# Self-attention of a decoder block: score tiles of half a PSUM bank for three of four heads, and two groups of heads projected together

## The chip, the cores and the metric

The kernel runs on one core of a Trainium2 chip. The metric is the device time of one execution in microseconds (us). TensorE (PE) multiplies matrices, VectorE (DVE) and ScalarE (ACT) read the products out of PSUM, GpSimd (POOL) and SyncE (SP) help with element-wise work and transfers. PSUM here is used as eight banks, each of 128 partitions by 512 fp32 values.

## The reference

One decoder block on x of shape (2, 1024, 256): self-attention with 16 heads of 16, cross-attention over 77 context rows, and a mixture of 8 experts. Only the self-attention is touched by the change:

```python
q, k, v = heads(xn @ Wq), heads(xn @ Wk), heads(xn @ Wv)     # xn = layernorm(x)
attn = softmax(einsum('bhqd,bhkd->bhqk', q, k) * e ** -0.5)
out = einsum('bhqk,bhkd->bhqd', attn + rel_bias, v)
x = x + layernorm(out) * gamma + beta
```

## The kernel before

All values are fp32. The kernel runs in stages: normalise and transpose x, the values and the part of the output that comes from the relative bias (`bias_o`), then the self-attention (about 90 to 710 us), the cross-attention, the routing and the experts.

Heads come in groups of four. A head has 16 values, and is padded to 32 rows (`wpad`), so four heads fill the 128 rows of TensorE's array: head `hh` of a group sits in rows 32·hh to 32·hh+31, its *row group*, and matmuls on different row groups can run beside each other. A unit is one group of one batch row, `u = 0..7`. `project(u, name)` makes its queries (`wqT`) and keys (`wkT`), 128 x 1024, with four matmuls of 512 columns each (L416), read out by ACT (L425) and DVE (L427). Row 16 of each head is 1 in the keys; in the queries it will hold minus the largest score, so that the second score matmul gives scores that are already shifted for the exponential.

A unit is worked in two halves of 512 queries (`halves`), and a half in eight steps. TensorE's order is written by hand: a loop over `n` in which stream A works on step `n` and stream B on step `m = n - LAG`, ten steps later.

- `stream_a(n, p)`: scores of 128 queries against 512 keys for heads 2p and 2p+1 (L443, two matmuls into a tile `sA` of two banks); DVE takes the maximum over the keys (L450).
- `shift_queries(h)`: after eight steps, four transposes into `pm` (L462), and DVE adds the negated maxima to the queries in place (L466).
- `stream_b(m, p)`: scores with keys as rows, 128 keys against 512 queries, for heads 2p and 2p+1 (L478), one bank `sB` each; ACT takes the exponential into `pt` (L488).
- `times_v(m)`: four matmuls (L499) that add the products with the values and with a row of ones into the bank `av`; it works on what stream B of the step before made.
- `collect(h)`: every eight steps, four transposes (L518) into `po`, division by the sum (L521, L522), and the bias part (L529). After the last group of a half `affine_residual` normalises.

There are 128 steps of A and 128 of B. In the 118 steps that hold both, the order on TensorE is A for heads 0, 1; B for heads 2, 3; B for heads 0, 1; A for heads 2, 3; then the products with the values. PSUM holds two `big` tiles of two banks (`sA`, and `pp` of the projections), three banks `one` (`sB`, `pm`, `po`) and one bank for `av`. The tile framework adds the waits: a matmul that reuses a bank waits until the reader of the old contents has finished, and a reader waits until TensorE's semaphore has counted far enough. TensorE has one such semaphore for all its readers.

Of the kernel before, what the change touches and what calls it, by code (L numbers as in the profile page):

```python
# [14 lines left out]
P = 128  # L15
# [22 lines left out]
def decoder_kernel(  # L38
# [36 lines left out]
        return psum.enter_context(tc.tile_pool(name=name, bufs=bufs, space=bass.MemoryType.PSUM))  # L75


    ps2, ps1, psav = banks("ps2a", 2), banks("ps1a", 3), banks("psav", 1)

    def big(name):  # L80
        return ps2.tile([P, 2, 512], F32, tag="big", name=name)

    pair = big

    def one(name):
        return ps1.tile([P, 512], F32, tag="one", name=name)

    flip = [0]

# [27 lines left out]
    def load_bcast(src, name):  # L117
# [4 lines left out]
    ident = const.tile([P, P], F32, name="ident")  # L122
    make_identity(nc, ident)

    onescol = const.tile([P, 1], F32, name="onescol")
    nc.vector.tensor_reduce(
        onescol, ident.rearrange("p (g r) -> p g r", r=32)[:, :, 16], AX.X, ALU.add
    )
    nhalf = const.tile([P, NT], F32, name="nhalf")
    nc.gpsimd.memset(nhalf, -0.5)  # L130

# [68 lines left out]
    fst = first.enter_context(tc.tile_pool(name="fst", bufs=1))  # L200

    wv = load_rows(a_wv, "wv", D, fst)
    wpad = {}
    for name, src in (("wq", a_wq), ("wk", a_wk)):
        raw = load_rows(src, f"{name}raw", D, fst)
        pad = at1.tile([P, 2, H, 32], F32, name=f"{name}pad")
        nc.gpsimd.memset(pad, 0.0)
        nc.gpsimd.tensor_copy(pad[:, :, :, 0:DH], raw.rearrange("p kc (h d) -> p kc h d", h=H))
        wpad[name] = pad.rearrange("p kc h r -> p kc (h r)")
    gamma_a = load_bcast(a_gamma, "gamma_a")  # L210
    beta_a = load_bcast(a_beta, "beta_a")

# [40 lines left out]
    vaug = at1.tile([P, QT, H, 32, B], F32, name="vaug")  # L253
    nc.gpsimd.memset(vaug, 0.0)
    nc.gpsimd.memset(vaug.rearrange("p k h r b -> p (k h) r b")[:, :, DH, :], 1.0)
    shifts = []
    for i in range(2):
        m = at1.tile([P, 4, NG, 32], F32, name=f"shift{i}")
        nc.gpsimd.memset(m, 0.0)
        shifts.append(m)  # L260

    for c in range(4):
        normalized_T(c, xnT[:, :, 512 * c : 512 * c + 512])
# [95 lines left out]
    evacuate(cxT.rearrange("p kc b t -> p kc (b t)"), pc[:, :, : B * T2])  # L359
    kbd = const.tile([P, 2, B, 4, T2], F32, name="kbd")  # L360
    for G in range(2):
        pk = one("pk")
        for kc in range(2):
            nc.tensor.matmul(
                pk[:, : B * T2],
                lhsT=cwk[:, kc, P * G : P * G + P],
                rhs=cxT[:, kc, :, :].rearrange("p b t -> p (b t)"),
                start=(kc == 0),
                stop=(kc == 1),
            )  # L370
        for j in range(4):
            nc.vector.tensor_scalar(
                kbd[:, G, :, j, :],
                pk[:, : B * T2].rearrange("p (b t) -> p b t", b=B),
                hsel[:, j : j + 1],
                None,
                ALU.mult,
            )
    vx = const.tile([P, B, H, 2, DH], F32, name="vx")
    nc.gpsimd.memset(vx, 0.0)  # L380
    for b in range(B):
        pv = one("pcv")
        for kc in range(2):
            nc.tensor.matmul(
                pv[:T2, :D],
                lhsT=cxT[:, kc, b, :],
                rhs=cwv[:, kc, :],
                start=(kc == 0),
                stop=(kc == 1),
            )  # L390
        for i in range(2):
            nc.vector.tensor_copy(
                vx[:T2, b, i::2, i, :],
                pv[:T2, :D].rearrange("p (h i d) -> p i h d", i=2, d=DH)[:, i, :, :],
            )
# [6 lines left out]

    halves = [(b, g, qb) for b in range(B) for g in range(NG) for qb in range(2)]
    units = {}
    outs = {}

    def project(u, name):
        b, g = u // NG, u % NG  # L410
        dst = at2.tile([P, S], F32, tag=f"{name}T", name=f"{name}T{u}", bufs=3)
        units[u, name] = dst
        pp = pair("pp")
        for half in range(2):
            for kc in range(2):
                nc.tensor.matmul(  # L416
                    pp[:, half, :],
                    lhsT=wpad[name][:, kc, P * g : P * g + P],
                    rhs=xnT[:, kc, b * S + 512 * half : b * S + 512 * half + 512],
                    start=(kc == 0),  # L420
                    stop=(kc == 1),
                )
        pf = pp.rearrange("p a f -> p (a f)")
        if name == "wq":
            nc.scalar.copy(dst, pf)  # L425
        else:
            nc.vector.tensor_scalar(dst, pf, onescol[:, 0:1], None, ALU.add)  # L427

    largest = {}

    def stream_a(n, p):
        h, r = n // 8, n % 8
        b, g, qb = halves[h]
        u = h // 2
        if (r, p) == (0, 0):
            largest[h] = at2.tile([P, 4, 4, 2], F32, tag="mx", name=f"mx{h}", bufs=3)
        qt, half = r // 2, r % 2
        qT, kT = units[u, "wq"], units[u, "wk"]
        s = pair("sA")
        for j in range(2):  # L440
            r0 = 32 * (2 * p + j)
            q0 = 512 * qb + P * qt
            nc.tensor.matmul(  # L443
                s[:, j, :],
                lhsT=qT[r0 : r0 + 32, q0 : q0 + P],
                rhs=kT[r0 : r0 + 32, 512 * half : 512 * half + 512],
                start=True,
                stop=True,
            )
        nc.vector.tensor_reduce(  # L450
            largest[h][:, qt, 2 * p : 2 * p + 2, half], s, AX.X, ALU.max
        )

    def shift_queries(h):
        b, g, qb = halves[h]
        shift = shifts[h % 2]
        nc.vector.tensor_reduce(
            shift[:, :, :, DH], largest.pop(h), AX.X, ALU.max, negate=True
        )
        pm = one("pm").rearrange("p (t f) -> p t f", f=P)  # L460
        for t in range(4):
            nc.tensor.transpose(  # L462
                pm[:, t, :], shift[:, t, :, :].rearrange("p h r -> p (h r)"), ident
            )
        qh = units[h // 2, "wq"][:, 512 * qb : 512 * qb + 512]
        nc.vector.tensor_tensor(qh, qh, pm.rearrange("p t f -> p (t f)"), ALU.add)  # L466

    powers = {}

    def stream_b(m, p):  # L470
        h, kt = m // 8, m % 8
        b, g, qb = halves[h]
        qT, kT = units[h // 2, "wq"], units[h // 2, "wk"]
        tiles = []
        for j in range(2):
            r0 = 32 * (2 * p + j)
            s = one("sB")
            nc.tensor.matmul(  # L478
                s,
                lhsT=kT[r0 : r0 + 32, kt * P : (kt + 1) * P],  # L480
                rhs=qT[r0 : r0 + 32, 512 * qb : 512 * qb + 512],
                start=True,
                stop=True,
            )
            tiles.append(s)
        for j, s in enumerate(tiles):
            pt = atp.tile([P, 512], F32, tag="pt", name="pt")
            nc.scalar.activation(pt, s, AF.Exp, scale=1.0 / 16.0)  # L488
            powers[m, 2 * p + j] = pt

    sums = {}

# [18 lines left out]
    def collect(h):  # L511
        b, g, qb = halves[h]
        if (b, qb) not in outs:
            outs[b, qb] = kp.tile([P, 4, D], F32, tag="o", name=f"o{b}{qb}", bufs=4)
        o, avs = outs[b, qb], sums.pop(h)
        po = one("po").rearrange("p (t f) -> p t f", f=P)
        for t in range(4):
            nc.tensor.transpose(po[:, t, :], avs[:, t * P : (t + 1) * P], ident)  # L518
        po = po.rearrange("p t (h r) -> p t h r", r=32)
        rs = small.tile([P, 4, 4], F32, tag="rs", name="rs")  # L520
        nc.vector.reciprocal(rs, po[:, :, :, DH])  # L521
        nc.vector.tensor_tensor(  # L522
            o[:, :, 64 * g : 64 * g + 64].rearrange("p t (h d) -> p t h d", h=4),
            po[:, :, :, 0:DH],
            rs.unsqueeze(3).to_broadcast([P, 4, 4, DH]),
            ALU.mult,
        )
        og = o[:, :, 64 * g : 64 * g + 64]
        nc.gpsimd.tensor_tensor(  # L529
            og, og, bias_o[:, b, 4 * qb : 4 * qb + 4, 64 * g : 64 * g + 64], ALU.add  # L530
        )
        if g == NG - 1:
            c = 2 * b + qb
            affine_residual(o, xs[:, 4 * c : 4 * c + 4, :], c, gamma_a, 1e-3)

    steps = 8 * len(halves)
    with tc.manual_schedule(engines={nc.tensor.engine}):
        for n in range(steps + LAG + 4):
            m = n - LAG
            if n == 0:  # L540
                project(0, "wq")
                project(0, "wk")
            if n % 16 == 11 and n // 16 + 1 < B * NG:
                project(n // 16 + 1, "wq")
            if n % 16 == 13 and n // 16 + 1 < B * NG:
                project(n // 16 + 1, "wk")
            if n % 8 == 1 and 8 < n < steps + 8:
                shift_queries(n // 8 - 1)
            if n < steps:
                stream_a(n, 0)  # L550
            if 0 <= m < steps:
                stream_b(m, 1)
                stream_b(m, 0)
            if n < steps:
                stream_a(n, 1)
            if 1 <= m <= steps:
                times_v(m - 1)
            if m % 8 == 2 and 0 < m < steps + 8 and m // 8 >= 1:
# [570 lines left out]
```

## Time and profile before

| | |
|---|---|
| time, median of 2 runs (lowest, highest) | 1391.63 us (1389.13, 1394.13) |
| time of the profiled execution | 1389.76 us |
| span of its profile | 1388.0 us |
| PE, DVE, ACT, POOL busy | 1182.9, 630.2, 460.1, 255.6 us |
| mean granted TensorE clock | 0.918 |

Each fp32 matmul leaves two records on PE, one for each of its passes; a transpose leaves one. PEld are the loads of the stationary operand. A record on PE lasts longer than the pass holds the array, since its end is the end of the last result; so records overlap, and a PE that looks busy all the time can still be waiting. Times of a stretch are given in us from the start of the span.

### The profile page before, as it was taken

The page shows a single profiled execution, that of the slowest core. Times are in us where ns is not written, and L with a number is a line of the kernel's source. Part 1 is how long each engine was busy: PE and PEld are TensorE (multiplying, and loading weights), DVE is VectorE, ACT ScalarE, POOL GpSimd, SP SyncE. Part 2 cuts the span into 40 slices and gives each one's busy share as a digit, 9 for nine tenths or more (in the row PEclk, how much of TensorE's full clock was granted, in tenths as well). Part 3 has the DMA queues.
Part 4 walks back from the last instruction along what each step waited for, and adds up shares of the span by engine and source line. Part 5 has one row for each costly group of instructions (what it writes and reads, how often), then busy time and mean ns, then how long its engine had stood idle before and what let it go on. Part 6 is the DMA issues. An engine that isn't in the chain of part 4 may idle for free. (4 is left out here: it accounts for less than half of the span.)

```text
span 1388.0 us, 15187 instructions
## 1 busy us (share of the span) xinstructions
PE 1182.9 (85%) x6231; PEld 632.9 (46%) x6231; DVE 630.2 (45%) x903; ACT 460.1 (33%) x801; POOL 255.6 (18%) x225
## 2 busy tenths in 40 slices
PE   0889999999989999999966678865999999999950
PEld 0533333332323233333213445634788888888840
DVE  6326565656565656566338565544300100100117
ACT  0100454545444455545531434310222222222210
POOL 7200000000000000000015554612222322222111
PEclk9995999999999999999997888765999999999985
DMA  7000000000000000000000000005244554455223
GB/s 167 9 1 0 1 1 1 1 1 0 1 0 1 0 1 0 1 0 1 0 0 1 0 11 5 31 16 182 68 148 154 180 186 155 161 196 165 97 72 110
DMA packets 62149, 73.95 MB, mean 53 GB/s; under 512 B 18059, under 2 KB 53504, under 8 KB 62080
## 3 DMA queue, kind: packets, MB, share of 16 engines
q1 hardware_dynamic: 55632, 60.56, 13.0%
q0 software_dynamic: 4960, 11.29, 2.7%
q10 hardware_dynamic: 1488, 1.13, 0.3%
q8 instruction: 49, 0.80, 0.2%
q14 instruction: 20, 0.16, 0.0%
HBM read 64.31 MB, written 10.22 MB: 54 GB/s over the span
## 5 line engine op out<-in xcount | busy, mean ns | idle before, releaser
L450 DVE TENSOR_REDUCE mx<-sA 128x2 f32<-128x1024 f32 x256 | 313.2, 1224 | 194.3 <-PE sB L478 103.7
L478 PE MATMUL sB<-wqT,wkT 32*128 32x512 f32 x1024 | 380.2, 639 | 5.4 <-ACT pt L488 5.4
L488 ACT ACTIVATE pt<-sB 128x512 f32<-128x512 f32 x512 | 278.3, 597 | 298.2 <-PE sB L478 269.7
L443 PE MATMUL sA<-wkT,wqT 32*128 32x512 f32 x1024 | 301.9, 684 | 10.1 <-DVE mx L450 6.7
L478 PEld LDWEIGHTS sB<-wqT,wkT 32*128 32x128 f32 x1024 | 120.6, 186 | 164.6 <-ACT pt L488 103.1
L1046 PE MATMUL po<-w,hT 128*128 128x256 f32 x736 | 168.1, 382 | 11.2 <-DVE y L1055 11.2
L1036 ACT ACTIVATE hT<-ph,b1s 128x256 f32<-128x256 f32 x184 | 87.3, 474 | 245.8 <-PE ph L1029 245.1
L1029 PE MATMUL ph<-xgT,w 128*128 128x256 f32 x736 | 163.2, 380 | 0.4 <-DVE xgT L1022 0.4
L1055 DVE TENSOR_SCALAR y<-po,by 128x256 f32<-128x256 f32 x46 | 20.1, 480 | 311.1 <-PE po L1046 311.1
L1046 PEld LDWEIGHTS po<-w,hT 128*128 128x128 f32 x736 | 138.1, 190 | 34.1 <-DVE y L1055 16.1
L1029 PEld LDWEIGHTS ph<-xgT,w 128*128 128x128 f32 x736 | 132.6, 189 | 27.4 <-ACT hT L1036 3.6
L499 PE MATMUL av<-pt,vaug 128*32 128x512 f32 x1024 | 137.8, 611 | 0.0
L443 PEld LDWEIGHTS sA<-wkT,wqT 32*128 32x128 f32 x1024 | 80.8, 194 | 115.8 <-issue 77.8
L529 POOL TENSOR_TENSOR o<-o,bias_o 128x256 f32<-128x256 f32 x16 | 11.6, 724 | 649.2 <-DVE o L522 649.2
L1058 POOL DMA_INDIRECT pairs<-y,to_row x46 | 46.4, 1008 | 148.4 <-DMA pairs<-y,to_row 97.5
L1004 POOL DMA_INDIRECT xg<-xnd,from_row x46 | 44.8, 975 | 150.1 <-PE px L1018 126.0
L499 PEld LDWEIGHTS av<-pt,vaug 128*32 128x32 f32 x1024 | 20.6, 109 | 97.6 <-issue 97.4
L166 PE MATMUL pxT<-ident,xn 128*128 128x128 f32 x96 | 19.8, 359 | 48.3 <-DVE xn L156 45.5
L633 PE MATMUL ppT<-ident,st 128*77 128x128 f32 x256 | 37.9, 310 | 17.2 <-POOL st L622 16.9
L634 ACT COPY PT<-ppT 77x1024 f32<-77x1024 f32 x32 | 31.1, 1008 | 43.8 <-PE ppT L633 43.8
L633 PEld LDWEIGHTS ppT<-ident,st 128*77 128x77 f32 x256 | 33.7, 171 | 25.0 <-POOL st L622 19.3
L615 POOL TENSOR_TENSOR st<-st,cm 128x1232 f32<-128x1232 f32 x16 | 36.1, 2259 | 47.9 <-DVE cs L621 18.1
(202 smaller groups left out, 958.6 us busy)
## 6 DMA issues: line engine op xcount, KB each, us to landing
w<-in_L_ffn_W_dram SPq DMA_DIRECT2D x46, 1024.0 KB, 8.4
yt<-pairs SPq DMA_DIRECT2D x8, 512.0 KB, 4.8
xs<-in_x_dram SPq DMA_DIRECT2D x4, 512.0 KB, 6.4
xnd<-xn SPq DMA_DIRECT2D x4, 512.0 KB, 2.8
out_dram<-acc SPq DMA_DIRECT2D x4, 512.0 KB, 3.0
xg<-xnd,from_row POOLq DMA_INDIRECT x46, 2.7
pairs<-y,to_row POOLq DMA_INDIRECT x46, 2.5
mk<-in_mask_BxSxS_ik_dram SPq DMA_DIRECT2D x1, 616.0 KB, 8.5
```

The lines of the kernel that those rows point to most:

```text
L443: nc.tensor.matmul(s[:, j, :], lhsT=qT[r0 : r0 + 32, q0 : q0 + P], rhs=kT[r0 : r0 + 32, 512 * half : 512 * half + 512], start=True, stop=True,
L450: nc.vector.tensor_reduce(largest[h][:, qt, 2 * p : 2 * p + 2, half], s, AX.X, ALU.max)
L478: nc.tensor.matmul(s, lhsT=kT[r0 : r0 + 32, kt * P : (kt + 1) * P], rhs=qT[r0 : r0 + 32, 512 * qb : 512 * qb + 512], start=True, stop=True,)
L488: nc.scalar.activation(pt, s, AF.Exp, scale=1.0 / 16.0)
L499: nc.tensor.matmul(sums[h][32 * hh : 32 * hh + 32, :], lhsT=vaug[:, kt, 4 * g + hh, :, b], rhs=powers.pop((m, hh)), start=(kt == 0), stop= ...
L615: nc.gpsimd.tensor_tensor(st, st, cm.unsqueeze(2).to_broadcast([P, H, T2]), ALU.subtract)
L633: nc.tensor.transpose(pp[:T2, h, :], st[:, 8 * G + h, :], ident)
L1004: nc.gpsimd.indirect_dma_start(out=xg[:, s, :], out_offset=None, in_=xnd[:, :], in_offset=bass.IndirectOffsetOnAxis(ap=from_row[:, 2 * i + ...
L1029: nc.tensor.matmul(ph[:, j, :], lhsT=w1[:, kc, hc * P : (hc + 1) * P], rhs=xgT[:, kc, :], start=(kc == 0), stop=(kc == 1),)
L1036: nc.scalar.activation(hT[:, hc, :], ph[:, j, :], AF.Gelu, bias=b1s[:, i, hc : hc + 1])
L1046: nc.tensor.matmul(po[:, s, :], lhsT=hT[:, hc, s * P : (s + 1) * P], rhs=w2[:, hc, :], start=(hc == 0), stop=(hc == NH - 1),)
L1058: nc.gpsimd.indirect_dma_start(out=pairs[:, :], out_offset=bass.IndirectOffsetOnAxis(ap=to_row[:, k : k + 1], axis=0), in_=y[:, s, :], in_ ...
```

## The change

1. **Projection.** `project(w, name, j)` serves two groups of heads at once (`w = 0..3`) in four pieces of 256 columns for the queries and four for the keys. The 32 rows of a row group hold one head of each of the two groups, 16 rows each (`wqk`). A piece is two matmuls of 256 columns. Queries are copied once (`qc`); of the keys DVE makes two copies, one for each group, in which the other group's rows are 0 but for one row of ones (`own`, `extra`). The eight pieces of the next `w` are spread over every second step of 16 steps in 32.
2. **Half banks.** One of the three banks `one` stays; the other two become `hb0` and `hb1`. `halfbank()` deals out their four halves of 256 columns in turn: first half of `hb0`, first half of `hb1`, second half of `hb0`, second half of `hb1`. Projection pieces, `pm`, `po` and most of stream B take their PSUM from there.
3. **Stream B.** For heads 1, 2 and 3 a score tile of 512 queries becomes two of 256 queries, with a matmul and an exponential each. Head 0 keeps the whole bank.
4. **Order.** The step's order on TensorE is written out as `turns`, in which A and B alternate matmul by matmul.
5. **Shift and collect** work in two parts of 256 columns. The shifted queries go to tiles of their own (`qB`) instead of in place.

```diff
-    ps2, ps1, psav = banks("ps2a", 2), banks("ps1a", 3), banks("psav", 1)
+    ps2, ps1, psh, psav = banks("ps2a", 2), banks("ps1a", 1), banks("psh", 1), banks("psav", 1)
+    halfbanks = [psh.tile([P, 512], F32, name=f"hb{i}") for i in range(2)]
+    turn_of = [0]
+    def halfbank(name):
+        k = turn_of[0] % 4
+        turn_of[0] += 1
+        return halfbanks[k % 2][:, 256 * (k // 2) : 256 * (k // 2) + 256]
...
-        pad = at1.tile([P, 2, H, 32], F32, name=f"{name}pad")
-        nc.gpsimd.memset(pad, 0.0)
-        nc.gpsimd.tensor_copy(pad[:, :, :, 0:DH], raw.rearrange("p kc (h d) -> p kc h d", h=H))
+        w = at1.tile([P, 2, 2, 4, 2, DH], F32, name=f"{name}2")
+        for kc in range(2):
+            for G in range(2):
+                nc.gpsimd.tensor_copy(
+                    w[:, kc, G],
+                    raw[:, kc, P * G : P * G + P].rearrange("p (i h d) -> p h i d", i=2, h=4),
+                )
...
+    def project(w, name, j):
+        b, G = w // 2, w % 2
+        cols = slice(256 * j, 256 * j + 256)
+        pp = halfbank("pp")
+        for kc in range(2):
+            nc.tensor.matmul(
+                pp,
+                lhsT=wqk[name][:, kc, P * G : P * G + P],
+                rhs=xnT[:, kc, b * S + 256 * j : b * S + 256 * j + 256],
+                start=(kc == 0),
+                stop=(kc == 1),
+            )
+        if name == "wq":
...
+            nc.scalar.copy(units[w, "q"][:, cols], pp)
+            return
+        for i in range(2):
...
+            nc.vector.tensor_scalar(
+                units[w, "k", i][:, cols], pp, own[i][:, 0:1], extra[i][:, 0:1], ALU.mult, ALU.add
+            )
...
+    def stream_b(m, hh, part):
+        h, kt = m // 8, m % 8
+        b, g, qb = halves[h]
+        r0 = 32 * hh
+        s, cols = (one("sB"), slice(0, 512)) if part is None else (halfbank("sB"), slice(256 * part, 256 * part + 256))
+        nc.tensor.matmul(
+            s,
+            lhsT=units[h // 4, "k", g % 2][r0 : r0 + 32, kt * P : (kt + 1) * P],
+            rhs=shifted[h][r0 : r0 + 32, cols],
+            start=True,
+            stop=True,
+        )
+        if (m, hh) not in powers:
+            powers[m, hh] = atp.tile([P, 512], F32, tag="pt", name="pt")
+        nc.scalar.activation(powers[m, hh][:, cols], s, AF.Exp, scale=1.0 / 16.0)
...
+    turns = [
+        ("a", 1), ("b", 2, 0), ("a", 0), ("b", 3, 0), ("b", 2, 1), ("a", 3), ("a", 2),
+        ("b", 1, 0), ("b", 0, None), ("b", 1, 1), ("b", 3, 1),
+    ]
...
+            w, r = n // 32, n % 32
+            if w + 1 < 2 * B and r in range(12, 28, 2):
+                project(w + 1, *pieces[(r - 12) // 2])
...
+            for t in turns:
+                if t[0] == "a" and n < steps:
+                    stream_a(n, t[1])
+                if t[0] == "b" and 0 <= m < steps:
+                    stream_b(m, *t[1:])
```

More of the change, by code (lines that the diff above doesn't have):

```diff
@@ L75, in banks @@
         return psum.enter_context(tc.tile_pool(name=name, bufs=bufs, space=bass.MemoryType.PSUM))
-    ps2, ps1, psav = banks("ps2a", 2), banks("ps1a", 3), banks("psav", 1)
+    ps2, ps1, psh, psav = banks("ps2a", 2), banks("ps1a", 1), banks("psh", 1), banks("psav", 1)
     def big(name):
         return ps2.tile([P, 2, 512], F32, tag="big", name=name)
-    pair = big
     def one(name):
         return ps1.tile([P, 512], F32, tag="one", name=name)
+    halfbanks = [psh.tile([P, 512], F32, name=f"hb{i}") for i in range(2)]
[4 more added lines that the diff above has]
+        return halfbanks[k % 2][:, 256 * (k // 2) : 256 * (k // 2) + 256]
     flip = [0]
@@ L123, in decoder_kernel @@
     make_identity(nc, ident)
[L125 to L128, printed above, removed]
+    own, extra, use = [], [], []
+    i32 = ident.rearrange("p (g r) -> p g r", r=32)
+    for i in range(2):
+        rows = [const.tile([P, 1], F32, name=f"{n}{i}") for n in ("own", "extra", "use")]
+        nc.vector.tensor_reduce(rows[0], i32[:, :, DH * i : DH * i + DH], AX.XY, ALU.add)
+        nc.vector.tensor_reduce(rows[1], i32[:, :, DH * (1 - i)], AX.X, ALU.add)
+        nc.vector.tensor_tensor(rows[2], rows[0], rows[1], ALU.add)
+        for all_, row in zip((own, extra, use), rows):
+            all_.append(row)
     nhalf = const.tile([P, NT], F32, name="nhalf")
@@ L202, in decoder_kernel @@
     wv = load_rows(a_wv, "wv", D, fst)
-    wpad = {}
+    wqk = {}
     for name, src in (("wq", a_wq), ("wk", a_wk)):
         raw = load_rows(src, f"{name}raw", D, fst)
-        pad = at1.tile([P, 2, H, 32], F32, name=f"{name}pad")
-        nc.gpsimd.memset(pad, 0.0)
-        nc.gpsimd.tensor_copy(pad[:, :, :, 0:DH], raw.rearrange("p kc (h d) -> p kc h d", h=H))
-        wpad[name] = pad.rearrange("p kc h r -> p kc (h r)")
+        w = at1.tile([P, 2, 2, 4, 2, DH], F32, name=f"{name}2")
[5 more added lines that the diff above has]
+                )
+        wqk[name] = w.rearrange("p kc g h i d -> p kc (g h i d)")
     gamma_a = load_bcast(a_gamma, "gamma_a")
@@ L255, in decoder_kernel @@
     nc.gpsimd.memset(vaug.rearrange("p k h r b -> p (k h) r b")[:, :, DH, :], 1.0)
-    shifts = []
+    shifts = {}
     for i in range(2):
-        m = at1.tile([P, 4, NG, 32], F32, name=f"shift{i}")
-        nc.gpsimd.memset(m, 0.0)
-        shifts.append(m)
+        for qb in range(2):
+            m = at1.tile([P, 4, NG, 32], F32, name=f"shift{i}{qb}")
+            nc.gpsimd.memset(m, 0.0)
+            shifts[i, qb] = m
     for c in range(4):
@@ L361, in decoder_kernel @@
     for G in range(2):
-        pk = one("pk")
+        pk = halfbank("pk")
         for kc in range(2):
@@ L381, in decoder_kernel @@
     for b in range(B):
-        pv = one("pcv")
+        pv = halfbank("pcv")
         for kc in range(2):
@@ L407, in decoder_kernel @@
     outs = {}
[L409 to L423, printed above, removed]
-        if name == "wq":
-            nc.scalar.copy(dst, pf)
-        else:
-            nc.vector.tensor_scalar(dst, pf, onescol[:, 0:1], None, ALU.add)
@@ L429, in decoder_kernel @@
-    largest = {}
-    def stream_a(n, p):
+    def project(w, name, j):
[10 more added lines that the diff above has]
+            )
+        if name == "wq":
+            if j == 0:
+                units[w, "q"] = at2.tile([P, S], F32, tag="qc", name=f"qc{w}")
+            nc.scalar.copy(units[w, "q"][:, cols], pp)
+            return
+        for i in range(2):
+            if j == 0:
+                units[w, "k", i] = at2.tile([P, S], F32, tag=f"kT{i}", name=f"kT{i}_{w}")
+            nc.vector.tensor_scalar(
+                units[w, "k", i][:, cols], pp, own[i][:, 0:1], extra[i][:, 0:1], ALU.mult, ALU.add
+            )
@@ L432, in stream_a @@
+    pieces = [("wk", 0), ("wq", 0), ("wk", 1), ("wk", 2), ("wk", 3), ("wq", 1), ("wq", 2), ("wq", 3)]
+    largest, tops = {}, {}
+    def stream_a(n, hh):
         h, r = n // 8, n % 8
         b, g, qb = halves[h]
-        u = h // 2
-        if (r, p) == (0, 0):
+        if h not in largest:
             largest[h] = at2.tile([P, 4, 4, 2], F32, tag="mx", name=f"mx{h}", bufs=3)
[L437 to L448, printed above, removed]
-            )
@@ L450, in stream_a @@
-        nc.vector.tensor_reduce(
-            largest[h][:, qt, 2 * p : 2 * p + 2, half], s, AX.X, ALU.max
-        )
+        qt, kh, p = r // 2, r % 2, hh // 2
+        if (n, p) not in tops:
+            tops[n, p] = [big("sA"), 0]
+        s = tops[n, p]
+        r0, q0 = 32 * hh, 512 * qb + P * qt
+        nc.tensor.matmul(
+            s[0][:, hh % 2, :],
+            lhsT=units[h // 4, "q"][r0 : r0 + 32, q0 : q0 + P],
+            rhs=units[h // 4, "k", g % 2][r0 : r0 + 32, 512 * kh : 512 * kh + 512],
+            start=True,
+            stop=True,
+        )
@@ L454, in shift_queries @@
+        s[1] += 1
+        if s[1] == 2:
+            nc.vector.tensor_reduce(
+                largest[h][:, qt, 2 * p : 2 * p + 2, kh], s[0], AX.X, ALU.max
+            )
+            del tops[n, p]
+    shifted = {}
     def shift_queries(h):
         b, g, qb = halves[h]
-        shift = shifts[h % 2]
+        i = g % 2
+        shift = shifts[i, qb]
         nc.vector.tensor_reduce(
-            shift[:, :, :, DH], largest.pop(h), AX.X, ALU.max, negate=True
+            shift[:, :, :, DH * (1 - i)], largest.pop(h), AX.X, ALU.max, negate=True
@@ L459, in shift_queries @@
         )
[L460 to L463, printed above, removed]
-            )
-        qh = units[h // 2, "wq"][:, 512 * qb : 512 * qb + 512]
-        nc.vector.tensor_tensor(qh, qh, pm.rearrange("p t f -> p (t f)"), ALU.add)
+        qh = at2.tile([P, 512], F32, tag="qB", name=f"qB{h}")
+        for u in range(2):
+            pm = halfbank("pm")
+            for t in range(2):
+                nc.tensor.transpose(
+                    pm[:, P * t : P * t + P],
+                    shift[:, 2 * u + t, :, :].rearrange("p h r -> p (h r)"),
+                    ident,
+                )
+            nc.vector.scalar_tensor_tensor(
+                qh[:, 256 * u : 256 * u + 256],
+                units[h // 4, "q"][:, 512 * qb + 256 * u : 512 * qb + 256 * u + 256],
+                use[i][:, 0:1],
+                pm,
+                ALU.mult,
+                ALU.add,
+            )
@@ L468, in decoder_kernel @@
+        shifted[h] = qh
     powers = {}
-    def stream_b(m, p):
+    def stream_b(m, hh, part):
         h, kt = m // 8, m % 8
         b, g, qb = halves[h]
[L473 to L489, printed above, removed]
+        r0 = 32 * hh
+        s, cols = (one("sB"), slice(0, 512)) if part is None else (halfbank("sB"), slice(256 * part, 256 * part + 256))
+        nc.tensor.matmul(
+            s,
+            lhsT=units[h // 4, "k", g % 2][r0 : r0 + 32, kt * P : (kt + 1) * P],
+            rhs=shifted[h][r0 : r0 + 32, cols],
+            start=True,
+            stop=True,
+        )
+        if (m, hh) not in powers:
+            powers[m, hh] = atp.tile([P, 512], F32, tag="pt", name="pt")
+        nc.scalar.activation(powers[m, hh][:, cols], s, AF.Exp, scale=1.0 / 16.0)
@@ L513, in collect @@
         if (b, qb) not in outs:
-            outs[b, qb] = kp.tile([P, 4, D], F32, tag="o", name=f"o{b}{qb}", bufs=4)
+            outs[b, qb] = kp.tile([P, 4, D], F32, tag="o", name=f"o{b}{qb}", bufs=3)
         o, avs = outs[b, qb], sums.pop(h)
[L516 to L519, printed above, removed]
         rs = small.tile([P, 4, 4], F32, tag="rs", name="rs")
[L521 to L527, printed above, removed]
+        for u in range(2):
+            po = halfbank("po").rearrange("p (t f) -> p t f", f=P)
+            for t in range(2):
+                c0 = P * (2 * u + t)
+                nc.tensor.transpose(po[:, t, :], avs[:, c0 : c0 + P], ident)
+            po = po.rearrange("p t (h r) -> p t h r", r=32)
+            t2 = slice(2 * u, 2 * u + 2)
+            nc.vector.reciprocal(rs[:, t2, :], po[:, :, :, DH])
+            nc.vector.tensor_tensor(
+                o[:, t2, 64 * g : 64 * g + 64].rearrange("p t (h d) -> p t h d", h=4),
+                po[:, :, :, 0:DH],
+                rs[:, t2, :].unsqueeze(3).to_broadcast([P, 2, 4, DH]),
+                ALU.mult,
+            )
         og = o[:, :, 64 * g : 64 * g + 64]
@@ L536, in decoder_kernel @@
     steps = 8 * len(halves)
+    turns = [
+        ("a", 1), ("b", 2, 0), ("a", 0), ("b", 3, 0), ("b", 2, 1), ("a", 3), ("a", 2),
+        ("b", 1, 0), ("b", 0, None), ("b", 1, 1), ("b", 3, 1),
+    ]
     with tc.manual_schedule(engines={nc.tensor.engine}):
+        for piece in pieces:
+            project(0, *piece)
         for n in range(steps + LAG + 4):
             m = n - LAG
[L540 to L546, printed above, removed]
+            w, r = n // 32, n % 32
+            if w + 1 < 2 * B and r in range(12, 28, 2):
+                project(w + 1, *pieces[(r - 12) // 2])
             if n % 8 == 1 and 8 < n < steps + 8:
                 shift_queries(n // 8 - 1)
[L549 to L555, printed above, removed]
+            for t in turns:
[3 more added lines that the diff above has]
+                    stream_b(m, *t[1:])
             if 1 <= m <= steps:
```

## The prediction

> **What bounds the kernel now.** I read the page first, then the waits, then one step of the attention in the timeline of each engine. The groups of the page show no full engine in the attention:
>
> ```profile
> L450 DVE TENSOR_REDUCE mx<-sA 128x2 f32<-128x1024 f32 x256 | 313.2, 1224 | 194.3 <-PE sB L478 103.7
> ...
> L488 ACT ACTIVATE pt<-sB 128x512 f32<-128x512 f32 x512 | 278.3, 597 | 298.2 <-PE sB L478 269.7
> ...
> L478 PEld LDWEIGHTS sB<-wqT,wkT 32*128 32x128 f32 x1024 | 120.6, 186 | 164.6 <-ACT pt L488 103.1
> ...
> L1036 ACT ACTIVATE hT<-ph,b1s 128x256 f32<-128x256 f32 x184 | 87.3, 474 | 245.8 <-PE ph L1029 245.1
> ```
>
> ACT and DVE idle as long as they work, and both wait for TensorE; TensorE's loads for B wait for ACT's exponentials. It is a ring: PE, ACT, PE. One plain step (118 of the 128 steps of each stream hold both) is this, PE first, then the loads, ACT and DVE:
>
> ```profile
> 564.75 0.70 PE L443 MATMUL sA<-wkT,wqT 32*128 32x512 f32 x2
> 564.77 0.70 PE L478 MATMUL sB<-wqT,wkT 32*128 32x512 f32 x2
> 565.29 0.59 PE L443 MATMUL sA<-wkT,wqT 32*128 32x512 f32 x2
> 565.30 2.01 PE L478 MATMUL sB<-wqT,wkT 32*128 32x512 f32 x5
> 566.63 0.70 PE L443 MATMUL sA<-wkT,wqT 32*128 32x512 f32 x2
> ...
> 567.69 1.06 PE L499 MATMUL av<-pt,vaug 128*32 128x512 f32 x8
> 568.68 0.70 PE L443 MATMUL sA<-wkT,wqT 32*128 32x512 f32 x2
> ...
> 565.72 0.18 PEld L478 LDWEIGHTS sB<-wqT,wkT 32*128 32x128 f32 x1 [0.24 <-issue]
> ...
> 566.62 0.18 PEld L478 LDWEIGHTS sB<-wqT,wkT 32*128 32x128 f32 x1 [0.72 <-ACT pt L488]
> ...
> 566.73 0.18 PEld L478 LDWEIGHTS sB<-wqT,wkT 32*128 32x128 f32 x1
> ...
> 565.97 1.57 ACT L488 ACTIVATE pt<-sB 128x512 f32<-128x512 f32 x3 [1.52 <-PE sB L478]
> ...
> 565.93 1.23 DVE L450 TENSOR_REDUCE mx<-sA 128x2 f32<-128x1024 f32 x1 [0.79 <-PE sB L478]
> ```
>
> The reader is to see the period, 568.68 - 564.75 = 3.93 us, in three rounds: A and B side by side from 564.75; B of head 0 alone, while head 1 waits for a bank until 566.62; head 1 with the other half of A; then the values, 0.99 us.
>
> **The prices, all from these rows.** A pass of 512 columns holds its row group 0.43 us (loads of the projection at 585.52, 585.95, 586.38), so a matmul 0.86; one of 256 columns half of that: in the experts 227 passes of 256 columns take 48.40 us, 0.213 each. A start after a wait costs 0.11 for the load (566.62 to 566.73). A result is there 0.16 after its pass leaves the array (record 0.587, pass 0.43). ACT starts 0.08 after the record's end (565.30 + 0.59 = 565.89; 565.97), PE goes on 0.05 after ACT's end (565.97 + 0.597 = 566.57; 566.62). From the last score to the values it takes 0.10.
>
> ```profile
> 1000.00:1050.00 50.00, 48.40 (x227) 40.82 (x227) 4.42 (x9) 13.58 (x29) 10.95 (x11) 1.00 0.41 145
> ```
>
> An exponential over 256 columns has no row. From below: 0.597 less half of what 512 more columns cost in ACT's copies (1012 - 586 = 426 ns, so 213): 0.384. From above: the 128x256 activation of the experts, 0.474. I take 0.384, as it is the same operation with fewer columns.
>
> **Where the new waits stand.** The built program says which instruction each wait is for. Every half-bank matmul waits for the reader of the *other* half of the same bank, two turns back: B of head 2, second half, waits for the exponential of its first half, though this lies in other columns. So hb0 and hb1 hold one live half each, and B has 2 x 256 + 512 columns in flight where it had 3 x 512. TensorE takes its matmuls in order, so whatever stands behind a waiting one waits too. And an exponential waits for a *count* of TensorE's one semaphore: the count for head 3, first half, includes A of head 0; that for head 1, first half, includes A of heads 3 and 2, which stand before it. (Of 1394 PE records from 150 to 390 us of the trace none ends before one issued earlier; I take counts to come in order too.)
>
> **The new step, from its first load at 0** (b2' is the first half of head 2, b2'' the second):
>
> ```
> a1, a0 (512) and b2', b3' (256)    array 0.11 to 0.96; counted at 1.12
> exp b2' 1.20 to 1.58               its own scores left the array at 0.53
> b2'' (waits for exp b2')           load 1.63, array 1.74 to 2.17; a3 beside it
> a2 (same row group, behind b2'')   2.17 to 3.02; counted at 3.18
> exp b1' (count holds a2)           3.26 to 3.65; b1' itself left at 2.60
> b3'' (same bank as b1')            load 3.70, array 3.80 to 4.23
> values                             4.33, next step's first load at 5.32
> ```
>
> 5.32 us against 3.93: +1.39. Behind b2'' stand all of A for heads 2, 3 and the rest of B; behind b3'' the values. ACT's seven operations (6 x 0.384 + 0.597 = 2.9 us) and DVE's two maxima (2.45) fit under 5.32 and cost nothing; under 3 us they would bound.
>
> **The sum.** Both streams: 118 x 1.39 = +164. Ten last steps with B alone (3.86 now, as 701.9 to 705.8 in the trace): two waits on ACT instead of one, about +0.45 each, +4. Projections: two units' work in one, so PE's part is halved. Now a step that holds one takes 7.56 instead of 3.93 (queries) or 7.95 instead of 4.51 (keys): 3.63 + 3.44 = 7.07 a unit, seven units inside the loop, 49. After: 24 pieces of 2 x 0.43 = 0.86 and some 0.2 for the change from row groups to the whole array and back, 25. So -24. The first one (before the loop): 8 x 0.86 against 8 x 0.86, 0. Shift and collect: the same transposes, one more wait each, 31 x 0.06 = +2. At 399 to 409 and 444 to 455 PE waits for DVE's normalisation; a slower step hides some of it: -2. POOL at the start: 8 copies of 128 columns (0.25 each, interpolated between its rows of 0.12 for 16 and 0.61 for 512 columns) for a memset and two copies (2.2), and two more shift memsets (0.55 each), ahead of the square roots that the first transposes wait for: +1. No transfer is added or moved; SP's queue is as it was. DVE's 48 extra copies of keys lie under its idle time. Sum +145: 1389.8 + 145 = 1535 us. The profiled execution lies 1.8 under the median of the runs shown; on the median's scale it is 1537. I say 1535.
>
> **Two rules weighed.** The trace shows no bank that one engine fills while another reads it, so of that there is no row. The Trainium skill (page "PSUM — Partial Sum Buffer", section "PSUM bank collisions raise a hardware error") says that PE writing and ACT reading one bank at once collide even in disjoint columns, and that waits go by bank and quadrant. That speaks against the change: by it the waits can't be dropped; without them the sum would be the last rival's. For the order of counts the row is the 1394 records above. The same page (section "Engine vs sequencer instructions") says that matmuls start and complete in program order; by it the sum stays at 1535, without it at 1500.
>
> **The rivals.**
>
> *Counts come early.* If a short matmul counts as soon as it is done, exp b2' can start at 0.77 (b2' and b3' make the two counts that it asks for): b2'' 1.31 to 1.74, a2 to 2.59, exp b1' 2.84 to 3.22, b3'' to 3.80, next step 4.89. +0.96 x 118 = 113, with the rest some 95 to 120 (steps around a projection piece shift the banks' turns and lose part of it): about 1500. For: nothing in the trace tests it, all scores being 512 wide. Against: a counter without order could release a reader too soon.
>
> *The step is longer still.* ACT's 0.474 for 256 columns adds 2 x 0.09 x 118 = +21: 1556. Half clock in parts of the stage: from 103 to 140 us, with A alone, the granted clock is 0.50; with B alone (655 to 705 us, two to three row groups at a time) it is 1.00. The new step keeps the array as busy as that tail (12 matmuls of 0.86 on a quarter of it in 5.32 us, 48%, against 8 in 3.86, 45%), so I expect full clock. Each tenth of the stage at half clock adds twelve steps with 3.4 us more of array time, +41. Together 1556 to 1620.
>
> *The waits are met before PE reaches them* (the other side). If b2'' and b3'' find their banks free, a row group has four slots of 0.43: 0.11 + 1.71 + 0.10 + 0.99 = 2.9 us, and DVE's 2.45 with its starts bounds at about 3.0. 118 x -0.93 - 24 + 5: about 1262. It decides from the point at which the step grows by less than 20 / 118 = 0.17 us, what the projections save. For: the row groups alone would allow it. Against: exp b2' would have to end before b2' itself has left the array; the chain above has 1.1 us there.
>
> **How the numbers follow.** Forecast (waits by bank, counts in order): 0.6. Counts early: 0.18. Longer still: 0.14. Other side: 0.05; the remaining 0.03 for a gain of the interleaving that cancels most of the loss. Likeliest 1535; the range is 1475 to 1595, from a little below the second case to inside the third. A measurement of this kernel tells about 2% (28 us) from no change: slower 0.92, within it 0.03, faster 0.05.
>
> **What would show it.** Right: a plain step of about 5.3 us from values to values; loads of `sB` in halves waiting for ACT twice in a step; the exponential of b2' starting with the end of A of heads 0, 1, not 0.24 after its own; PE's idle before loads up, ACT's idle up by about 140 us; in projections PE's time halved. Wrong: a period under 4.1; an exponential over 256 columns that starts while a 512-wide matmul issued earlier still runs (counts early); a granted clock below 1 between 150 and 700 us; waits for DVE in place of ACT.

## The result, and the profile after

The changed kernel takes 1628.68 us (median of 2 runs, 1628.39 to 1628.98) against 1391.63: a ratio of 1.170, 95% interval 1.161 to 1.179. It is slower, as forecast, but by 237 us where 143 were forecast, and 1628 lies above the range.

The groups of its page, for the lines that answer to those shown of before (busy us, mean ns, then the idle time ahead of the group and what ended it):

```profile
L521 PE MATMUL hb<-qB,kT 32*128 32x256 f32 x1536 | 457.4, 477 | 74.0 <-ACT pt L530 69.1
L480 DVE TENSOR_REDUCE mx<-sA 128x2 f32<-128x1024 f32 x256 | 313.0, 1224 | 336.2 <-PE sA L471 290.2
L530 ACT ACTIVATE pt<-hb 128x256 f32<-128x256 f32 x768 | 281.7, 384 | 463.4 <-PE sA L471 275.6
...
L521 PEld LDWEIGHTS hb<-qB,kT 32*128 32x128 f32 x1536 | 219.2, 205 | 309.3 <-ACT pt L530 270.9
```

Loads of B's half tiles wait 270.9 us for exponentials (103.1 before), and exponentials wait 275.6 us for `sA`, a tile that they don't read: that is the count. An exponential over 256 columns takes 384 ns. One plain step at full clock, in the timeline of all engines, gives the places:

```profile
734.10 0.69 PE L471 MATMUL sA<-kT,qc 32*128 32x512 f32 x1
...
734.11 0.48 PE L521 MATMUL hb<-qB,kT 32*128 32x256 f32 x1
...
734.12 0.69 PE L521 MATMUL hb<-qB,kT 32*128 32x256 f32 x3
...
734.63 0.60 PE L471 MATMUL sA<-kT,qc 32*128 32x512 f32 x2
735.30 0.66 ACT L530 ACTIVATE pt<-hb 128x256 f32<-128x256 f32 x2 [1.71 <-PE sA L471]
...
735.74 0.18 PEld L521 LDWEIGHTS hb<-qB,kT 32*128 32x128 f32 x1 [1.32 <-ACT pt L530]
...
736.01 0.48 PE L521 MATMUL hb<-qB,kT 32*128 32x256 f32 x1
...
736.33 0.37 PE L521 MATMUL hb<-qB,kT 32*128 32x256 f32 x1
736.47 0.38 ACT L530 ACTIVATE pt<-hb 128x256 f32<-128x256 f32 x1 [0.51 <-PE hb L521]
...
736.70 0.59 PE L471 MATMUL sA<-kT,qc 32*128 32x512 f32 x1
...
737.37 0.38 ACT L530 ACTIVATE pt<-hb 128x256 f32<-128x256 f32 x1 [0.52 <-PE sA L471]
...
737.80 0.29 PEld L521 LDWEIGHTS hb<-qB,kT 32*128 32x128 f32 x2 [0.61 <-ACT pt L530]
...
738.43 1.07 PE L540 MATMUL av<-pt,vaug 128*32 128x512 f32 x8
```

The next step's first load is at 739.43: a period of 5.33 us. But in stretches of the loop the clock is halved (last columns of the windows: granted clock, DMA share, GB/s):

```profile
200.00:250.00 50.00, 45.95 (x278) 20.96 (x282) 23.08 (x26) 23.59 (x63) 0.72 (x1) 1.00 0.00 1
300.00:350.00 50.00, 45.29 (x198) 18.04 (x191) 16.54 (x19) 15.97 (x43) 0.72 (x1) 0.62 0.00 1
900.00:950.00 50.00, 46.06 (x166) 17.41 (x162) 5.75 (x21) 18.31 (x51) 1.91 (x2) 0.50 0.00 0
```

The reader is to see that PE looks as busy in the second window as in the first, with 198 records in place of 278. In before, the window in which PE waits for the normalisation and the one with the tail (the last ten steps, B alone) were:

```profile
400.00:450.00 50.00, 45.62 (x242) 14.57 (x235) 29.54 (x43) 21.26 (x38) 2.59 (x3) 0.90 0.00 1
650.00:700.00 50.00, 47.30 (x267) 13.75 (x260) 19.99 (x22) 28.15 (x52) 1.45 (x2) 1.00 0.00 1
```

At half clock the changed kernel's products with the values start at 313.88 and 322.92 in the timeline, a step of 9.04 us.

From here on "the loop" is the time from the first product with the values to the last, and half clock is added up from the trace's clock records within it: 13.7 us of 571.7 before, 222.9 us of 806.6 after. Ahead of the loop the change costs 3.5 us (first projection at 93.9 us instead of 90.4); behind it 1 us.

### The profile page after: what moved, and what is told of

The parts are those of the page before. It is cut to its first block, busy times and chain, and to the rows that moved or that the text cites. A ratio compares the mean times of both kernels' runs of the same rounds, so it can differ in the third digit from the quotient of the medians.

```text
span 1627.3 us, 17406 instructions
## 1 busy us (share of the span) xinstructions
PE 1356.7 (83%) x6999; PEld 769.5 (47%) x6999; DVE 642.0 (39%) x980; ACT 511.6 (31%) x1193; POOL 255.5 (16%) x231
## 5 line engine op out<-in xcount | busy, mean ns | idle before, releaser
L521 PE MATMUL hb<-qB,kT 32*128 32x256 f32 x1536 | 457.4, 477 | 74.0 <-ACT pt L530 69.1
L530 ACT ACTIVATE pt<-hb 128x256 f32<-128x256 f32 x768 | 281.7, 384 | 463.4 <-PE sA L471 275.6
L471 PE MATMUL sA<-kT,qc 32*128 32x512 f32 x1024 | 391.2, 715 | 6.6 <-DVE mx L480 6.6
L521 PEld LDWEIGHTS hb<-qB,kT 32*128 32x128 f32 x1536 | 219.2, 205 | 309.3 <-ACT pt L530 270.9
L471 PEld LDWEIGHTS sA<-kT,qc 32*128 32x128 f32 x1024 | 142.1, 209 | 111.5 <-DVE mx L480 61.2
L540 PE MATMUL av<-pt,vaug 128*32 128x512 f32 x1024 | 173.0, 756 | 0.0
L521 PE MATMUL sB<-qB,kT 32*128 32x512 f32 x256 | 161.5, 713 | 0.0
L530 ACT ACTIVATE pt<-sB 128x512 f32<-128x512 f32 x128 | 75.9, 593 | 5.3 <-PE sB L521 4.8
```

Of the source, the lines that this page charges most:

```text
L471: nc.tensor.matmul(s[0][:, hh % 2, :], lhsT=units[h // 4, "q"][r0 : r0 + 32, q0 : q0 + P], rhs=units[h // 4, "k", g % 2][r0 : r0 + 32, 512 ...
L521: nc.tensor.matmul(s, lhsT=units[h // 4, "k", g % 2][r0 : r0 + 32, kt * P : (kt + 1) * P], rhs=shifted[h][r0 : r0 + 32, cols], start=True, ...
L530: nc.scalar.activation(powers[m, hh][:, cols], s, AF.Exp, scale=1.0 / 16.0)
L540: nc.tensor.matmul(sums[h][32 * hh : 32 * hh + 32, :], lhsT=vaug[:, kt, 4 * g + hh, :, b], rhs=powers.pop((m, hh)), start=(kt == 0), stop= ...
```

## The experiments

| kernel | time us | plain step us | loop us | half clock in it |
|---|---|---|---|---|
| before | 1391.6 | 3.93 | 571.7 | 13.7 |
| changed | 1628.7 | 5.33 | 806.6 | 222.9 |
| projection alone, whole banks, old order | 1368.3 | 3.93 | 551.5 | 13.7 |
| whole banks, interleaved order | 1361.2 | 3.90 | 550.3 | 20.5 |
| half banks, old order | 1599.1 | 5.16 | 778.1 | 173.9 |
| half banks, B ahead of A | 1467.3 | 4.23 | 646.7 | 80.1 |
| three half banks | 1497.1 | 4.70 | 677.3 | 76.6 |
| before with two banks for B | 1488.3 | 4.42 | 666.7 | 75.8 |
| changed, gaps filled | 1581.2 | 5.33 | 757.1 | 81.8 |

The plain step is the commonest distance from one step's products with the values to the next step's. The kernels with one run (B ahead of A, three half banks, two banks) stand beside runs of before at 1391.8, 1389.6 and 1389.6 us on their chips.

**1. The projection alone.** The two groups' projection, shift and collect of the change, on the banks and in the order of before:

```diff
-    ps2, ps1, psh, psav = banks("ps2a", 2), banks("ps1a", 1), banks("psh", 1), banks("psav", 1)
+    ps2, ps1, psav = banks("ps2a", 2), banks("ps1a", 3), banks("psav", 1)
...
     def halfbank(name):
-        k = turn_of[0] % 4
-        ...
+        return one(name)[:, :256]
...
+    turns = [("a", 0), ("a", 1), ("b", 2, None), ("b", 3, None), ("b", 0, None), ("b", 1, None), ("a", 2), ("a", 3)]
```

> Only the projection of two groups together (with its pieces and the two-part shift and collect) is kept; B's score tiles are three whole banks again and the step's order is that of the kernel before. Theory (the loss is the waits for half-filled banks, and the half clock that follows from them): plain step 3.93 us as before, the loop from the first to the last product with the values 546 us against 572, about 1373 us in all, clock at full speed in the loop. Rival (the projection of two groups is itself what costs, by its waits in between and its double copies of the keys): 1400 us or more.

Measured: 1368.33 us, ratio 0.983 (0.979 to 0.987); step 3.93, loop 551.5. The time lies 5 us under the expected 1373; a step with a projection piece takes 4.99 us, 1.06 more than a plain one. The projection gains what was forecast for it, and the rival falls. The loop keeps the 13.7 us at half clock that before has.

**2. The interleaved order on whole banks.** As the last, with `turns` = a1, b2, a0, b3, a3, a2, b1, b0.

> As the projection alone, but with the interleaved order of the change (a1, b2, a0, b3, a3, a2, b1, b0), on whole banks. Theory: plain step 3.90 us, about 1371 us in all, since a whole bank frees in time. Rival (the interleaved order costs, since an exponential waits for the count of A's matmuls in front of it): a step of 4.5 us or more, 1440 us or more.

Measured: 1361.21 us, ratio 0.978 (0.974 to 0.982). Two rows of the timeline of PE, one step apart:

```profile
361.88 1.07 PE L534 MATMUL av<-pt,vaug 128*32 128x512 f32 x8
...
365.78 1.07 PE L534 MATMUL av<-pt,vaug 128*32 128x512 f32 x8
```

3.90 us, as expected; the total is 10 us under the expected 1371. The order is harmless where three whole banks stand behind it. This version takes less time than both kernels, though whether as much as 2% less than before is not settled (0.974 to 0.982), nor that it beats the one of experiment 1, since their intervals overlap.

**3. Half banks in the old order.** The changed kernel with another list:

```diff
+    turns = [("a", 0), ("a", 1), ("b", 2, 0), ("b", 3, 0), ("b", 2, 1), ("b", 3, 1),
+             ("b", 0, None), ("b", 1, 0), ("b", 1, 1), ("a", 2), ("a", 3)]
```

> The changed kernel with its half banks, but the step's order is that of the kernel before, with the halves of a pair of heads side by side (a0, a1, b2', b3', b2'', b3'', b0, b1', b1'', a2, a3). Theory (half banks cost, whatever the order): at full clock a plain step of 5.2 us, and the clock falls in parts of the loop as in the changed kernel, 1560 to 1620 us. Rival (the interleaved order is needed for the loss): step about 3.9 us, 1400 us or less.

Measured: 1599.09 us (ratio 1.150, 1.142 to 1.157), step 5.16, half clock for 173.9 us. With experiments 1 and 2 this makes a square: whole banks 3.93 and 3.90, half banks 5.16 and 5.33. The half banks cost in both of these orders; the interleaving adds little.

**4. B ahead of A.** Half banks as in the change; B's first halves stand before A of heads 1 and 0, and b1' before A of heads 3 and 2:

```diff
+    turns = [("b", 2, 0), ("b", 3, 0), ("a", 1), ("a", 0), ("b", 2, 1), ("b", 1, 0),
+             ("a", 3), ("a", 2), ("b", 0, None), ("b", 1, 1), ("b", 3, 1)]
```

> The changed kernel with half banks as they are, but in each step B's first two halves stand before A of heads 1 and 0, and B of head 1, first half, before A of heads 3 and 2; nothing else is moved. Theory (an exponential waits for the count of every matmul issued before its own): exponentials start 0.4 to 0.9 us sooner, plain step 4.31 us instead of 5.32; loop 614 us at full clock, 1441 us, and up to 60 us more if the clock still falls. Rival (only the sharing of banks counts, the order does not): step 5.3 us, 1535 us or more.

Measured: 1467.3 us, 26 over the expected 1441 and within its allowance for the clock; step 4.23. In the changed kernel the exponential of b2' started 1.20 us after the step's first load; here the timeline of PE has the first load's matmul at 365.67,

```profile
365.67 0.48 PE L521 MATMUL hb<-qB,kT 32*128 32x256 f32 x2
```

and that of ACT the exponential:

```profile
366.40 0.66 ACT L530 ACTIVATE pt<-hb 128x256 f32<-128x256 f32 x2 [1.09 <-PE hb L521]
```

It starts 0.73 us after that first load, and it waits for `hb`, no longer for `sA`. So 1.10 of the 1.40 us that a step grew hang on the order: on which matmuls of A are counted ahead of a half tile's exponential. They hang on it because the next half tile waits for that exponential: in experiment 2 the same interleaving costs nothing.

**5. A third bank in halves.** Head 0's scores are cut as well, and six halves go round over three banks (the lines that drop the whole bank are left out):

```diff
-    halfbanks = [psh.tile([P, 512], F32, name=f"hb{i}") for i in range(2)]
+    halfbanks = [psh.tile([P, 512], F32, name=f"hb{i}") for i in range(3)]
...
-        k = turn_of[0] % 4
+        k = turn_of[0] % 6
...
-        return halfbanks[k % 2][:, 256 * (k // 2) : 256 * (k // 2) + 256]
+        return halfbanks[k % 3][:, 256 * (k // 3) : 256 * (k // 3) + 256]
...
-        ("b", 1, 0), ("b", 0, None), ("b", 1, 1), ("b", 3, 1),
+        ("b", 1, 0), ("b", 0, 0), ("b", 0, 1), ("b", 1, 1), ("b", 3, 1),
```

> The changed kernel with a third bank dealt out in halves too: head 0's scores are also two tiles of 256 queries, and the six halves go round over three banks, so that a matmul waits for the reader of three turns back instead of two. Theory (the wait for the same bank's other half sets the step): plain step at full clock 4.7 us in place of 5.3, loop 644 us, 1470 us, and up to 40 us more for half clock in the tail. Rival (the number of pieces costs: now eight score matmuls and eight exponentials of B in a step instead of seven): step 5.4 us or more, 1640 us or more.

Measured: 1497.05 us. The timeline of PE:

```profile
402.63 1.07 PE L540 MATMUL av<-pt,vaug 128*32 128x512 f32 x8
...
407.33 1.07 PE L540 MATMUL av<-pt,vaug 128*32 128x512 f32 x8
```

4.70 us with one tile and one exponential more in each step. So the number of pieces is not what made the step long; how many turns back the waited-for reader lies counts for more. Three live halves are 3 x 256 = 768 columns in flight, fewer than the 1024 of the changed kernel, and the step is shorter even so: the columns in flight do not set it alone. The total is 27 us over the expected 1470, within the allowance for the tail, which ran at half clock for 56 us.

**6. Two banks for B in the kernel before.** One number changed:

```diff
-    ps2, ps1, psav = banks("ps2a", 2), banks("ps1a", 3), banks("psav", 1)
+    ps2, ps1, psav = banks("ps2a", 2), banks("ps1a", 2), banks("psav", 1)
```

> The kernel before, unchanged but for B's banks: two in place of three, the freed one unused. B then has 1024 columns in flight, as many as live at once in the changed kernel, without halves, new order or new projection. Theory (what is in flight sets the step): plain step 4.42 us instead of 3.93, loop 634 us, 1458 us, and a clock that stays up, since the array idles less than in the changed kernel. Rival (a bank less is hidden, since ACT is idle half of the time): 1395 us.

Measured: 1488.29 us, and in the timeline of PE

```profile
363.48 1.07 PE L499 MATMUL av<-pt,vaug 128*32 128x512 f32 x8
...
367.90 1.07 PE L499 MATMUL av<-pt,vaug 128*32 128x512 f32 x8
```

4.42 us, as worked out: a third less in flight costs 0.49 us a step, without halves, pieces or a new order. With 1024 columns in flight too, half banks take 5.33 in the changed order and 4.23 in that of experiment 4, above and below this 4.42: with few columns in flight the order decides. That the clock would stay up was half wrong. It stayed up while both streams ran (17 of 601 us at half clock), but in the last ten steps, with B alone, it fell (59 of 66 us), and these steps took 7.11 us. That is most of the 30 us over the expected 1458.

**7. The gaps filled.** In each step of the changed kernel with both streams three matmuls of A are computed twice, the first time in the gaps:

```diff
+    turns = [("a", 1), ("b", 2, 0), ("a", 0), ("b", 3, 0), ("f", 3), ("f", 2), ("b", 2, 1), ("a", 3), ("a", 2),
+             ("b", 1, 0), ("b", 0, None), ("b", 1, 1), ("f", 0), ("b", 3, 1)]
...
+                if t[0] == "f" and LAG <= n and n + (t[1] == 0) < steps:
+                    filler(n + (t[1] == 0), t[1])   # stream_a's matmul into the same tile, without the maximum
```

> The changed kernel, with useless matmuls put into the two gaps of each step in which both streams run: A of heads 3 and 2 is computed once more while B of head 2 waits, and A of head 0 of the next step once more before B's last half; the real A overwrites them. The gaps lie behind waits that they don't lengthen. Theory (the clock is halved because the array idles for 0.8 us twice a step): the granted clock in the loop goes up to 0.95 or more, plain step stays 5.3 us, loop 717 us and 1544 us in all, so more work takes less time than the changed kernel's 1628 us. Rival (the clock is halved by something else: the number of loads or of switches, or the power): clock 0.86 or lower, 1635 us or more.

Measured: 1581.21 us, ratio 1.136 to before (1.130 to 1.142) against 1.170 of the changed kernel. Three of the same windows:

```profile
200.00:250.00 50.00, 49.71 (x328) 23.89 (x330) 23.39 (x26) 23.27 (x62) 0.72 (x1) 1.00 0.00 1
300.00:350.00 50.00, 49.58 (x330) 22.48 (x326) 24.51 (x27) 23.53 (x63) 0.72 (x1) 1.00 0.00 1
850.00:900.00 50.00, 46.14 (x166) 17.40 (x162) 5.76 (x21) 18.23 (x51) 1.91 (x2) 0.50 0.00 0
```

More work takes 47 us less. While both streams run, 17 of 692 us are at half clock, in place of 162 of 742; the step stays 5.33, and the mean granted clock of the loop is 0.95 in place of 0.86. The last steps, where nothing was filled in, are the control: 65 of 65 us at half clock, 6.67 us a step, as in the changed kernel. More loads and more work went with more full clock, so neither of them halves it; the fillers raised how much of the array is in use, in the gaps above all. Which stretches count is worked out below. The total misses the expected 1544 by 37 us: 21 us are that tail, which the expectation had at full clock, the 17 us at half clock are about 7, and steps with a piece of the keys' projection about 6 (12 of them at 6.86 us, where the changed kernel has 6.39); the last few us stay open.

## Why the prediction was right or wrong

**The chain of the new step held at every link on its path.** Us from the step's first load:

```
                       predicted   measured
exponential of b2'       1.20        1.20
load of b2''             1.63        1.64
exponential of b1'       3.26        3.27
load of b3''             3.70        3.70
values                   4.33        4.33
next step                5.32        5.33
```

The duration of an exponential over 256 columns was taken from the lower end, 0.384, and is 0.384. One link that is not on the path was wrong: b1' does not stand behind a2 but starts as soon as its own row group is free (below).

**The small terms held.** The projection: 6.39 - 5.33 = 1.06 us for a piece, as taken, and experiment 1 shows it by itself, with the whole kernel about 23 us faster. Shift and collect: 6.10 and 5.94 against 5.33, so 0.77 and 0.61 where before they cost 0.58 each; 31 x 0.11 = 3 us for the 2 of the sum. The start cost 3.5 us instead of 1. One reading ahead of the sum is loose, and nothing rests on it: DVE does not idle as long as it works, its maxima are busy for 313.2 us behind 194.3 us of idle time.

**What failed is the clock, the term set to zero.** The step that failed is the sentence that the new step "keeps the array as busy as that tail", so that full clock was expected and half clock stood in the sum with nothing. Measured, the loop ran at half clock for 222.9 us. It grew by 234.9 us, of which the chain and the small terms explain about 144 (571.7 + 144 = 716); 91 are left. At half clock a step takes 9.04 instead of 5.33, so each us at half clock loses 1 - 5.33 / 9.04 = 0.41, and 222.9 - 13.7 = 209 us lose about 86 (an estimate, by the plain step's price). The price was right (3.7 us a step; the rival had 3.4), and the mechanism stood among the rivals with a chance of 0.14, but the amount was not: the loop spent 28% of its time at half clock, and the rival's upper end, 1620, counted on about two tenths.

The comparison that misled was one of means: 48% of the array in use against 45% in the old tail. The trace's clock records change in steps of 3.41 us, and over a sliding window of that length the use, worked out from the records of PE (a quarter of the array for each pass of 32 rows or 32 columns, 0.427 us for 512 columns, twice that at half clock), never falls under 0.60 in the plain steps of before and under 0.37 in its tail, but to 0.31 in the changed kernel's step, in which nothing is in the array for about 0.8 us before b2'' and 0.5 us before b3''. With the fillers it stays at 0.44 or more.

The clock records show more when the loops of all nine kernels are cut into stretches of 3.41 us, on the grid on which each trace's clock records begin. Of the stretches at full clock, all 42 with a use under 0.36 were followed by half clock, and none of the 1368 with 0.43 or more; of the 120 between them 29 were. Of the 66 stretches at half clock that were followed by full clock, 65 had 0.64 or more. So by these traces it is the use within one such stretch that goes with the clock, and not the mean of the step; where the border lies between 0.36 and 0.43 this working does not show. It also fits that the changed kernel lost the clock only in places: what a stretch catches of the two gaps changes from stretch to stretch, and from 184.8 to 287.2 us the clock stayed full.

Before had the same in small. Its 13.7 us at half clock come behind the stretches from 406.5 us (use 0.29) and 454.3 us (0.23), where PE waits for the normalisation. So the sign "a granted clock below 1 between 150 and 700 us" was there before the change too (0.90 in the window from 400), and the profile of before held a row for the price of a gap, which the prediction did not use.

The tail of the changed kernel, which the sum had at 4.3 us a step, ran at 6.67 (27 us more than before's tail instead of 4); a step of it at full clock takes 4.23, as one in experiment 7 does.

**The rivals.** *Counts come early* is out: the exponential of b2' waits until 735.30, 0.07 after the end of A's last record (734.63 + 0.60), though the last record of the first halves ends at 734.81; experiment 4 moves it by moving A. *The step is longer still* is what happened, by the clock alone and not by ACT's 0.474: the chance of 0.14 stood at the right cause with too small an amount. *The waits are met before PE reaches them* is out by the loads' waits above. The Trainium skill's rule of one bank and quadrant (page "PSUM — Partial Sum Buffer", section "PSUM bank collisions raise a hardware error"), which spoke against the change, agrees with what the built program waits for: b2'' is loaded at 735.74, only after the exponential of b2' (735.30 + 0.38), which reads other columns. Experiment 5 puts a number on these waits: 0.63 us a step for one bank more between reader and writer. Whether halves could be used without the waits was not tried.

## What to carry to other kernels

Cutting a PSUM tile in half gives no second buffer as long as reader and writer are kept apart by bank; it halves what that bank has in flight, and the ring PE, ACT, PE gets longer. Where engines wait on a shared count, what is issued ahead of a producer belongs to its latency; put short producers that somebody waits for first. And when a change opens gaps in TensorE, price them twice, once as waits and once for the clock, by the emptiest few microseconds rather than the mean.

## What the runs showed of the hardware

Matmuls on different row groups start out of program order, and by the ends that the profile models they end out of it too, though the count keeps to it. In the changed kernel b1' was issued after a2; its load is at 736.01 and its last record ends at 736.33 + 0.37 = 736.70, where a2's second pass only starts. Its exponential still begins at 737.37, 0.08 after a2's end (736.70 + 0.59). The trace's times of TensorE's count say the same: 736.45, where b2'' ends, then nothing until 737.30, 737.35 and 737.39, one behind the other. The Trainium skill (page "PSUM — Partial Sum Buffer", section "Engine vs sequencer instructions") says that matmuls start and complete in program order; for starts and ends of matmuls on separate row groups these rows say otherwise, for the count they agree.

Useless work can save time: three more matmuls a step took 47 us off, with the plain step at 5.33 us as before and half clock down from 222.9 to 81.8 us of the loop.
